# The forward scan moved to the end of the order, with an opening that starts by chunks

## The chip, the cores and the metric

One Trainium2 chip, one of its cores. The metric is the device time of one launch in microseconds, taken as the median of several runs; the profile is one further execution of the same program.

## The reference, cut to what matters

Four images of 4096 tokens with 128 channels go through two layers. The first is a state-space block with three scans over the tokens of an image: in forward order (0), backwards (1), and in an order of 16 interleaved slices (2). Each scan has 256 channels with 16 states, and its steps are sequential in time. The second layer is an attention block with 16 heads of 8 channels, then a feed-forward part and a mixture of 64 experts that each pick 8 tokens.

```python
def step(h, inp):
    u_, de_, b_, c_ = inp
    dA = jnp.exp(de_[..., None] * A)
    h = h * dA + (de_ * u_)[..., None] * b_[:, None, :]
    y = jnp.einsum('bdn,bn->bd', h, c_)
    return (h, y)
...
y = y_f + y_b + y_s
out = jnp.einsum('od,bdl->blo', out_proj_w, y)
...
x = x + _L0_conv_ref(_gn(x), ...)
t = _to_tokens(x)
t = t + _L1_attn_ref(_ln_t(t), ...)
t = t + _L1_ffn_ref(_ln_t(t), ...)
```

What matters for the change: the attention of an image needs all of its tokens, and each token needs the sum of the three scans at its place. A forward scan gives its tokens in rising order, a backward one in falling order, and the sliced one gives in each piece some tokens from all over the image.

## The kernel before, in words

The order of the work is written out by hand: Python generators issue instructions bit by bit and are advanced in turn[...]. A `Pace` advances a chain of generators by a share per turn; `flow` runs several pieces a few turns apart; `Bank` hands out a PSUM buffer (one in the main loops).

- `Inputs` makes, for each image and order, four chunks of 1024 tokens of delta, u, B and C, and the gate silu(z) (`d_sz`); it stores them in HBM. `pieces` sets the order: 0, 1, 2, with the slices laid out ahead of order 2.
- `Scans.of_image` (L488 on) runs the scan of one image in 384 steps: 3 orders x 4 chunks x 8 groups of 32 channels x 4. A step loads delta and du (L520, on SP), takes an exponential on ACT (`exp`, L534), and on DVE a product, the scan and a second product (`inputs` L541, `step` L550 and L555). Every four steps PE sums over the states (`total`, L582), and `out` (L598) adds D u and stores the group to the image's `d_y` of that order: one store on POOL for order 0 (L601), four for the others (L607, L611; for order 2 they scatter over the image). Loads are issued two steps ahead. `product` (L571 to L576) makes du for a coming chunk on the side.
- `Attention.opening` turns the sums of the scans into what the attention needs. `tokens` (L773 on) takes 512 tokens: it loads for each half of the channels the three sums and the gate (L789, on SP), adds and multiplies them on DVE (L794), multiplies by the output weights on PE (`out`, L802), adds x (L807), normalizes (`norm`, L836 to L842) and takes angles. `heads` takes the sine (L867) and `rings` makes products along a head (L879 to L886), transposes them on PE (`qT`, L894), splits them (L897, L898) and stores six parts of q on SP (L902). An opening has eight such groups of 512 tokens.
- `Attention.loop` is the attention of one image in 1024 rounds. A round has 4 score matmuls (L955), 2 exponentials of 128x1024 on ACT (L960) and 4 matmuls with the values (L969; the trace shows each as two). Behind each round it calls `beside(i)`.
- `Attention.after` closes an image: output projection, norms, feed-forward, gate logits. `settle` (L824) leaves turns empty, in number by `lag`.

The stages follow each other so. First the inputs of all images with the scan of image 0 beside them. Then the opening of image 0 in a wide form. Then the loops of images 0, 1 and 2: beside the rounds of image b, `beside` advances the scan of image b + 1 (`following`), then `after` of image b - 1 (`last`), and then, when the scan of image b + 1 is over (`left == 0.0`), the opening of image b + 1 (`opens`). What is left of the opening at the end of the loop runs in the `while not last.done or not opens.done` loop without attention rounds beside it. Last comes the loop of image 3 with the closes and the experts beside it, and the end of the experts.

In `beside`, `left` is 2.1 times the steps that the scan still has, and the scan's share per round is `left` over the rounds to 860, held between 0.5 and 1.3. While `left` is over 0, `lag` is 2 and the other work takes PE's bank only in rounds in which the scan issued an exponential and no sum (`slot`).

Of the kernel before, what the change touches and what calls it, by code (L numbers as in the profile page):

```python
# [11 lines left out]
F32 = mybir.dt.float32  # L12
# [8 lines left out]
DI = 256  # L21
NS = 16
R = 8
SLICES = 16
T = 1024
NC = L // T
NS2 = NS // 2
# [58 lines left out]
WAIT = "wait"  # L86
# [39 lines left out]
class Bank:  # L126


    def __init__(self, pool, n):
        self.pool, self.free = pool, n  # L130
# [78 lines left out]

def early(b, order, c):  # L210

    return b == 0 or (b == 1 and order == 0 and c < 2)


def decays(nc, dirs, ws, inputs):
# [12 lines left out]
class Inputs:  # L228
# [38 lines left out]
    def pieces(self, images):  # L267

        for b in images:
            self.sz[b] = self.dram.tile([DI, L], F32, name=f"d_sz_{b}")  # L270
            yield self.norm(b)
            for order in range(3):
                if order == 2:
                    yield self.slices(b)
                for c in range(NC):
                    yield self.of_chunk(b, order, c)
                    third, at = divmod(order * NC + c, 3)
                    if at == 2:
                        yield self.gate(b, third)

# [183 lines left out]
class Scans:  # L464
# [6 lines left out]
    def __init__(self, tc, ctx, ws, ident, bank, dram):  # L471
        nc = self.nc = tc.nc
        self.ws, self.bank, self.dram = ws, bank, dram
        const = ctx.enter_context(tc.tile_pool(name="s_const", side="right", bufs=1))
        self.rows = ctx.enter_context(tc.tile_pool(name="s_rows", side="right", bufs=2))
        self.deep = ctx.enter_context(tc.tile_pool(name="s_deep", side="right", bufs=3))
        self.small = ctx.enter_context(tc.tile_pool(name="s_small", side="right", bufs=2))

        self.sel = const.tile([P, 2, 32], F32, name="sel")
        nc.vector.memset(self.sel, 0.0)  # L480
        for i in range(2):
            nc.vector.tensor_reduce(
                self.sel[:, i, 16 * i : 16 * i + 16], ident.rearrange("p (d n) -> p d n", n=NS2),
                mybir.AxisListType.X, ALU.add,
            )
        self.sums, self.steps, self.did = {}, {}, set()

    def of_image(self, b, made, alone=False):  # L488

        nc = self.nc  # L490
        self.steps[b] = 0
        for order in range(3):
            self.sums[b, order] = self.dram.tile([DI, L], F32, name=f"d_y_{b}_{order}")
        steps = [(order, c, k, j) for order in range(3) for c in range(NC) for k in range(8) for j in range(4)]
        spread, ends, tiles = {}, {}, {}

        def rows_of(order, c, q):
# [61 lines left out]
        def product(s):  # L559

            order, c, k, j = steps[s]
            part, turn = divmod(4 * k + j - 8, 3)
            chunk = (b, order, c + 1) if c + 1 < NC else (b, order + 1, 0) if order < 2 else (b + 1, 0, 0)
            if part < 0 or turn == 1 or chunk not in made or early(*chunk):
                return
            of, m, at = made[chunk], part // 4, part % 4 * (T // 4)
            cut = slice(m * P, (m + 1) * P), slice(at, at + T // 4)
            if turn == 0:
                for name in ("delta", "u"):
                    t = self.extra.tile([P, T // 4], F32, tag=f"x_{name}", name=f"x_{name}_{b}_{s}")  # L570
                    nc.sync.dma_start(out=t, in_=of[name][cut])  # L571
                    tiles["x", name] = t
            else:
                t, u = tiles.pop(("x", "delta")), tiles.pop(("x", "u"))
                nc.vector.tensor_mul(t, t, u)  # L575
                nc.gpsimd.dma_start(out=of["du"][cut], in_=t)  # L576
# [10 lines left out]
        def out(s, y):  # L587

            order, c, k, j = steps[s]
            u = tiles.pop(("u", s - 3))  # L590
            o = self.rows.tile([P, T // 4], F32, tag="o", name=f"o_{b}_{s}")
            y = y[:, : T // 4]
            into = o[:, ::-1] if order == 1 else o
            if order == 2:

                into = o.rearrange("p (i j) -> p j i", i=SLICES)
                u, y = (t.rearrange("p (j i) -> p j i", i=SLICES) for t in (u, y))
            nc.vector.scalar_tensor_tensor(into, u, self.ws[order]["D"][:, k : k + 1], y, ALU.mult, ALU.add)  # L598
            to = self.sums[b, order][32 * k : 32 * k + 32]
            if order == 0:  # L600
                nc.gpsimd.dma_start(out=to[:, c * T : (c + 1) * T].rearrange("p (g t) -> g p t", g=4), in_=o)  # L601
                return
            for g in range(4):
                rows = o[32 * g : 32 * g + 32]
                if order == 1:
                    end = L - c * T - g * (T // 4)
                    nc.gpsimd.dma_start(out=to[:, end - T // 4 : end], in_=rows)  # L607
                else:
                    n = T // 4 // SLICES
                    at = (4 * c + g) * n  # L610
                    nc.gpsimd.dma_start(  # L611
                        out=to.rearrange("p (i j) -> p i j", i=SLICES)[:, :, at : at + n],
                        in_=rows.rearrange("p (i j) -> p i j", i=SLICES),
                    )
# [29 lines left out]
        for s in range(n):  # L644
            if s + self.AHEAD < n:
                yield from have(s + self.AHEAD)
            turn = s % 4 if s >= 4 else None
# [34 lines left out]
class Attention:  # L682

    def __init__(self, tc, ctx, w, gate, cols, ident, bank, dram, t1, w_out, sums, sz, x):
        nc = self.nc = tc.nc
        gate_w, gate_b = gate
        self.tc, self.cols, self.ident, self.bank, self.dram, self.t1 = tc, cols, ident, bank, dram, t1
        self.w_out, self.sums, self.sz, self.x = w_out, sums, sz, x  # L690
        const = ctx.enter_context(tc.tile_pool(name="a_const", bufs=1))
        self.half_pi = column(nc, const, math.pi / 2.0, "a_half_pi")

# [79 lines left out]
    def tokens(self, b, g, angles):  # L773


        nc = self.nc
        xin = self.x[b].rearrange("(t p) c -> p t c", p=P)
        to = self.t1[b].rearrange("(t p) c -> p t c", p=P)
        cut, tiles = slice(g * 512, (g + 1) * 512), slice(g * 4, g * 4 + 4)
        x_g = self.piece([P, 4, C], "x_g", name=f"xr_{b}_{g}")  # L780
        nc.sync.dma_start(out=x_g, in_=xin[:, tiles, :])
        ys = []
        for m in range(2):
            rows = slice(m * P, (m + 1) * P)
            parts = []
            for i, src in enumerate([self.sums[b, order] for order in range(3)] + [self.sz[b]]):
                tag, bufs = ("y0", 2 * self.n) if i == 0 else (f"p{i - 1}", self.ahead)
                t = self.one.tile([P, 512], F32, tag=tag, bufs=bufs, name=f"y{i}_{b}_{g}_{m}")
                nc.sync.dma_start(out=t, in_=src[rows, cut])  # L789
                parts.append(t)  # L790
            yield
            y = parts[0]
            for t, op in zip(parts[1:], (ALU.add, ALU.add, ALU.mult)):
                nc.vector.tensor_tensor(y, y, t, op)  # L794
            ys.append(y)
# [659 lines left out]
def tile_kernel(tc, ctx, x, in_proj_w, dirs, out_proj_w, attn, gate, weight1, weight2, out):  # L1455


    nc = tc.nc
# [26 lines left out]
                first.run(1.0)  # L1485
            others.rest()
    bank = scans.bank = Bank(ctx.enter_context(tc.tile_pool(name="bank", bufs=1, space=PSUM)), 1)
    block = Attention(tc, ctx, attn, gate, cols, ident, bank, dram, t1, w_out, scans.sums, inputs.sz, x)

    following = Pace(*(scans.of_image(b, inputs.made) for b in range(1, nb)))  # L1490
    with ExitStack() as wide:
# [11 lines left out]
    with tc.manual_schedule():  # L1503
        last = Pace()
        n = 3 * NC * NB
        for b in range(nb - 1):
            opens = Pace(block.opening(b + 1))

            def beside(i):

                left = 2.1 * (n + 1 - scans.steps.get(b + 1, 0))
                block.lag = 2 if left > 0.0 else 0
                scans.did.clear()
                following.run(min(1.3, max(0.5, left / max(1, 860 - i))))
                other = last if not last.done else opens if left == 0.0 else None
                if other is None:
                    return
                slot = left == 0.0 or "exp" in scans.did and "sum" not in scans.did
                if other.then is not PE or not bank.free:
                    other.run(1.0)  # L1520
                    slot = slot and left > 0.0
                if slot and other.then is PE and bank.free:
                    other.run(1.0)

            block.loop(b, beside)
            while not last.done or not opens.done:
                ready = scans.steps.get(b + 1, 0) > n
                if not last.done or ready:
                    (opens if last.done else last).run(1.0)
                following.run(0.5 if ready else 1.0)  # L1530
            last = Pace(block.after(b))
        following.rest()
# [69 lines left out]
```

## Time and profile before

| | us |
|---|---|
| median of 3 runs | 11980.78 (11979.94 to 11983.56) |
| profiled execution, its own time | 11985.97 |
| its span, first to last instruction | 11984.3 |
| PE busy | 10801.0 (90%) |
| ACT busy | 10457.4 (87%) |
| DVE busy | 8666.3 (72%) |
| POOL busy | 3068.7 (26%) |
| L960, exponentials of the attention, 8192 | 7778.6 busy |
| L969, matmuls with the values, 32768 | 5681.9 busy |
| mean granted TensorE clock | 0.950 |

Busy time is the union of an engine's instructions; [...] A line such as "PE out L802 <- DVE o L598" in a list of waits says that PE stood ahead of the `out` matmul of L802 until the DVE instruction of L598 was done; where several things were awaited, the last to end is named.

### The profile page before, as it was taken

The numbers are of one execution on the slowest core, as the hardware profiler recorded it, in microseconds if no ns is written. First come the engines' busy times: TensorE is split into PE (matmuls) and PEld (weight loads), VectorE is DVE, ScalarE is ACT, GpSimd is POOL, SyncE is SP. The second block draws the span as 40 slices with busy tenths as digits, with TensorE's granted clock in tenths as the row PEclk, the third lists the DMA queues.
The fourth block names the chain that finished last, engine by engine and source line by source line (L and its number), as shares of the span: only waits on it lengthen the run. The fifth ranks groups of instructions, "written<-read, shape, count | busy, mean of one in ns | idle before, by whom it ended". The sixth has DMA issues, their size and how long they took to land.

```text
span 11984.3 us, 184513 instructions
## 1 busy us (share of the span) xinstructions
PE 10801.0 (90%) x69190; PEld 3648.6 (30%) x69190; DVE 8666.3 (72%) x8841; ACT 10457.4 (87%) x10884; POOL 3068.7 (26%) x4017
## 2 busy tenths in 40 slices
PE   7898888489999999899999998999999999999995
PEld 3333333222222222233333222233332223333323
DVE  6999999889888877898889878989898321101123
ACT  5776777389999999899999988999999999999992
POOL 2323243222232322323334223233232110100011
PEclk9898989699999999999999999999999999999997
DMA  5666666655656565665565655655555332222125
GB/s 159 206 185 181 188 177 187 199 159 151 157 150 158 136 163 162 166 158 151 145 152 141 158 169 165 156 147 148 144 144 134 123 109 67 74 69 78 61 71 182
DMA packets 835831, 1747.64 MB, mean 146 GB/s; under 512 B 141070, under 2 KB 373574, under 8 KB 834678
## 3 DMA queue, kind: packets, MB, share of 16 engines
q1 hardware_dynamic: 649438, 1318.65, 41.5%
q0 software_dynamic: 144000, 307.48, 8.2%
q10 hardware_dynamic: 41496, 109.71, 3.5%
q8 instruction: 543, 8.90, 0.3%
q14 instruction: 354, 2.90, 0.1%
HBM read 1379.76 MB, written 355.47 MB: 145 GB/s over the span
## 4 chain that ended last, share of the span: by engine, by line
PE 62%; ACT 12%; issue 9%; DVE 8%; DMA 7%; SPq 1%; POOL 0%; ACTq 0%; DVEq 0%; POOLq 0%
PE acc L969 31%; PE s L955 15%; ACT e L960 7%; PE y L582 5%; DVE h L550 3%; PE cv L390 3%; PE sp L448 3%; DMA delta<-d_delta 2%; PE fo L1118 1%; PE xd L404 1%; PE h L1107 1%; DMA y<-d_y 1%; DVE dB L541 1%; ACT dA L534 1%; ACT delta L534 1%
## 5 line engine op out<-in xcount | busy, mean ns | idle before, releaser
L960 ACT ACTIVATE e<-s 128x1024 f32<-128x1024 f32 x8192 | 7778.6, 1102 | 366.5 <-PE s L955 322.0
L969 PE MATMUL acc<-e,val 128*32 128x512 f32 x32768 | 5681.9, 614 | 79.7 <-ACT av L978 79.0
L955 PE MATMUL s<-qm,key 32*128 32x512 f32 x16384 | 2783.4, 501 | 373.2 <-ACT e L960 311.5
L955 PEld LDWEIGHTS s<-qm,key 32*128 32x128 f32 x16384 | 1067.2, 183 | 3628.7 <-issue 1953.2
L552 POOL COPY ends<-h 128x1 f32<-128x1 f32 x1152 | 1299.0, 1130 | 2685.2 <-DVE h L550 2682.1
L969 PEld LDWEIGHTS acc<-e,val 128*32 128x32 f32 x32768 | 1027.7, 109 | 2007.6 <-issue 1015.7
L550 DVE TENSOR_TENSOR_SCAN h<-delta,ends,du 128x1024 f32<-128x1024 f32 x576 | 1349.6, 2343 | 113.8 <-ACT delta L534 95.9
L550 DVE TENSOR_TENSOR_SCAN h<-dA,ends,dB 128x1024 f32<-128x1024 f32 x576 | 1349.6, 2343 | 46.5 <-ACT dA L534 43.4
L541 DVE TENSOR_TENSOR dB<-du,B 128x1024 f32<-128x1024 f32 x768 | 927.8, 1208 | 603.2 <-PE y L582 387.4
L534 ACT ACTIVATE dA<-delta,A 128x1024 f32<-128x1024 f32 x768 | 938.0, 1221 | 176.9 <-DMA delta<-d_delta 169.8
L534 ACT ACTIVATE delta<-delta,A 128x1024 f32<-128x1024 f32 x768 | 939.0, 1223 | 132.7 <-PE y L582 124.6
L541 DVE TENSOR_TENSOR du<-du,B 128x1024 f32<-128x1024 f32 x768 | 920.4, 1198 | 30.4 <-DMA B<-d_bc 30.4
L555 DVE TENSOR_TENSOR du<-h,C 128x1024 f32<-128x1024 f32 x768 | 934.6, 1217 | 0.1
L555 DVE TENSOR_TENSOR dB<-h,C 128x1024 f32<-128x1024 f32 x768 | 934.2, 1216 | 0.0
L582 PE MATMUL y<-dB,sel 128*32 128x256 f32 x6144 | 724.3, 394 | 33.4 <-DVE ring L879 20.8
L582 PE MATMUL y<-du,sel 128*32 128x256 f32 x6144 | 718.1, 390 | 12.6 <-DVE du L555 12.5
L390 PE MATMUL cv<-xn,conv 128*128 128x512 f32 x1024 | 487.9, 629 | 32.5 <-DVE xn L325 17.3
L984 POOL DMA_DIRECT2D d_ctx<-av x512 | 260.1, 520 | 926.9 <-ACT av L978 920.2
L611 POOL DMA_DIRECT2D d_y<-o x512 | 329.5, 674 | 521.0 <-DVE o L598 470.7
L550 DVE TENSOR_TENSOR_SCAN h<-delta,du 128x1024 f32<-128x1024 f32 x192 | 438.2, 2282 | 19.6 <-ACT delta L534 11.0
L550 DVE TENSOR_TENSOR_SCAN h<-dA,dB 128x1024 f32<-128x1024 f32 x192 | 438.2, 2282 | 16.7 <-ACT dA L534 15.1
L576 POOL DMA_DIRECT2D d_du<-x_delta x272 | 154.7, 569 | 1104.4 <-DVE x_delta L575 1033.8
(260 smaller groups left out, 7862.8 us busy)
## 6 DMA issues: line engine op xcount, KB each, us to landing
delta<-d_delta SPq DMA_DIRECT2D x768, 512.0 KB
du<-d_du SPq DMA_DIRECT2D x576, 512.0 KB
du<-d_du ACTq DMA_DIRECT2D x192, 512.0 KB
key<-d_q SPq DMA_DIRECT2D x352, 256.0 KB
d_u<-u POOLq DMA_DIRECT2D x48, 1024.0 KB, 5.6
B<-d_bc SPq DMA_DIRECT2D x96, 512.0 KB
C<-d_bc SPq DMA_DIRECT2D x96, 512.0 KB
d_delta<-r POOLq DMA_DIRECT2D x48, 1024.0 KB, 5.5
```

Of the source, the lines that this page charges most:

```text
L390: nc.tensor.matmul(ps[:, cut], w["conv"][:, k, m * P : (m + 1) * P], reads(k, g), start=(k == 0), stop=(k == 3))
L448: nc.tensor.matmul(ps[:, cut], sign, t[:, m, cut], start=(i == 0), stop=(i == 2))
L534: nc.scalar.activation(tiles["delta", s], t, AF.Exp, scale=A)
L541: nc.vector.tensor_mul(tiles["du", s], du, spread[order, c, "B", j % 2])
L550: nc.vector.tensor_tensor_scan(h, dA, dB, first, ALU.mult, ALU.add)
L552: nc.gpsimd.tensor_copy(ends[order, c][:, at : at + 1], h[:, T - 1 :])
L555: nc.vector.tensor_mul(dB, h, spread[order, c, "C", j % 2])
L582: nc.tensor.matmul(y[32 * g : 32 * g + 32, : T // 4], self.sel[:, j // 2, :], hC[:, 256 * g : 256 * g + 256], start=(j == 0), stop=(j == 3),)
L611: nc.gpsimd.dma_start(out=to.rearrange("p (i j) -> p i j", i=SLICES)[:, :, at : at + n], in_=rows.rearrange("p (i j) -> p i j", i=SLICES),)
L955: nc.tensor.matmul(s_ps[:, k, :], keys[f"{i // 4}"][rows, cut].bitcast(F32R), queries[j, qb][rows, :].bitcast(F32R), start=True, stop=True,)
L960: nc.scalar.activation(e, s_ps, AF.Exp, scale=1.0 / math.sqrt(D))
L969: nc.tensor.matmul(accs[j, qb][32 * k : 32 * k + 32, :], v[:, k * VW : k * VW + 32], es[i][k // 2][:, k % 2, :], start=(kc == 0), stop=(kc ...
```

## The change

The order of the three scans becomes 1, 2, 0 everywhere: in the inputs, in the steps, in what `product` prepares, and in `early`. The forward scan stores each chunk of 1024 tokens in a DRAM tile of its own. `Scans` counts the groups for which `out` was issued (`stored`), and `tokens` leaves turns empty until, for its chunk c of the forward scan, two groups beyond that chunk were issued (or all 96). It then loads the sums in the order 1, 2, 0, and leaves `settle(2)` turns empty between loads and adds. In `beside` the opening may run as soon as `last` is done, where it had to wait for the end of the scan, and the rounds in which the scan is paced become 890 for 860. Each store, load, matmul and vector operation is there as often as before; line numbers after line 25 shift, by 11 at the end.

```diff
--- before.py
+++ after.py
@@ -22,6 +22,7 @@
 NS = 16
 R = 8
 SLICES = 16
+ORDERS = 1, 2, 0
 T = 1024
 NC = L // T
 NS2 = NS // 2
@@ -209,7 +210,7 @@
 
 def early(b, order, c):
 
-    return b == 0 or (b == 1 and order == 0 and c < 2)
+    return b == 0 or (b == 1 and order == ORDERS[0] and c < 2)
 
 
 def decays(nc, dirs, ws, inputs):
@@ -269,12 +270,12 @@
         for b in images:
             self.sz[b] = self.dram.tile([DI, L], F32, name=f"d_sz_{b}")
             yield self.norm(b)
-            for order in range(3):
+            for turn, order in enumerate(ORDERS):
                 if order == 2:
                     yield self.slices(b)
                 for c in range(NC):
                     yield self.of_chunk(b, order, c)
-                    third, at = divmod(order * NC + c, 3)
+                    third, at = divmod(turn * NC + c, 3)
                     if at == 2:
                         yield self.gate(b, third)
 
@@ -483,15 +484,17 @@
                 self.sel[:, i, 16 * i : 16 * i + 16], ident.rearrange("p (d n) -> p d n", n=NS2),
                 mybir.AxisListType.X, ALU.add,
             )
-        self.sums, self.steps, self.did = {}, {}, set()
+        self.sums, self.steps, self.stored, self.did = {}, {}, {}, set()
 
     def of_image(self, b, made, alone=False):
 
         nc = self.nc
-        self.steps[b] = 0
-        for order in range(3):
+        self.steps[b] = self.stored[b] = 0
+        for order in range(1, 3):
             self.sums[b, order] = self.dram.tile([DI, L], F32, name=f"d_y_{b}_{order}")
-        steps = [(order, c, k, j) for order in range(3) for c in range(NC) for k in range(8) for j in range(4)]
+        for c in range(NC):
+            self.sums[b, 0, c] = self.dram.tile([DI, T], F32, name=f"d_y_{b}_0_{c}")
+        steps = [(order, c, k, j) for order in ORDERS for c in range(NC) for k in range(8) for j in range(4)]
         spread, ends, tiles = {}, {}, {}
 
         def rows_of(order, c, q):
@@ -560,7 +563,8 @@
 
             order, c, k, j = steps[s]
             part, turn = divmod(4 * k + j - 8, 3)
-            chunk = (b, order, c + 1) if c + 1 < NC else (b, order + 1, 0) if order < 2 else (b + 1, 0, 0)
+            turn_of = ORDERS.index(order) + 1
+            chunk = (b, order, c + 1) if c + 1 < NC else (b, ORDERS[turn_of], 0) if turn_of < 3 else (b + 1, ORDERS[0], 0)
             if part < 0 or turn == 1 or chunk not in made or early(*chunk):
                 return
             of, m, at = made[chunk], part // 4, part % 4 * (T // 4)
@@ -596,10 +600,12 @@
                 into = o.rearrange("p (i j) -> p j i", i=SLICES)
                 u, y = (t.rearrange("p (j i) -> p j i", i=SLICES) for t in (u, y))
             nc.vector.scalar_tensor_tensor(into, u, self.ws[order]["D"][:, k : k + 1], y, ALU.mult, ALU.add)
+            self.stored[b] += 1
+            if order == 0:
+                to = self.sums[b, order, c][32 * k : 32 * k + 32]
+                nc.gpsimd.dma_start(out=to.rearrange("p (g t) -> g p t", g=4), in_=o)
+                return
             to = self.sums[b, order][32 * k : 32 * k + 32]
-            if order == 0:
-                nc.gpsimd.dma_start(out=to[:, c * T : (c + 1) * T].rearrange("p (g t) -> g p t", g=4), in_=o)
-                return
             for g in range(4):
                 rows = o[32 * g : 32 * g + 32]
                 if order == 1:
@@ -683,11 +689,11 @@
 
 
 
-    def __init__(self, tc, ctx, w, gate, cols, ident, bank, dram, t1, w_out, sums, sz, x):
+    def __init__(self, tc, ctx, w, gate, cols, ident, bank, dram, t1, w_out, scans, sz, x):
         nc = self.nc = tc.nc
         gate_w, gate_b = gate
         self.tc, self.cols, self.ident, self.bank, self.dram, self.t1 = tc, cols, ident, bank, dram, t1
-        self.w_out, self.sums, self.sz, self.x = w_out, sums, sz, x
+        self.w_out, self.scans, self.sums, self.sz, self.x = w_out, scans, scans.sums, sz, x
         const = ctx.enter_context(tc.tile_pool(name="a_const", bufs=1))
         self.half_pi = column(nc, const, math.pi / 2.0, "a_half_pi")
 
@@ -777,18 +783,23 @@
         xin = self.x[b].rearrange("(t p) c -> p t c", p=P)
         to = self.t1[b].rearrange("(t p) c -> p t c", p=P)
         cut, tiles = slice(g * 512, (g + 1) * 512), slice(g * 4, g * 4 + 4)
+        c, part = divmod(g, T // 512)
+        while self.scans.stored[b] < min(8 * (2 * NC + c + 1) + 2, 8 * 3 * NC):
+            yield WAIT
+        srcs = [(self.sums[b, 1], cut), (self.sums[b, 2], cut), (self.sums[b, 0, c], slice(part * 512, part * 512 + 512))]
         x_g = self.piece([P, 4, C], "x_g", name=f"xr_{b}_{g}")
         nc.sync.dma_start(out=x_g, in_=xin[:, tiles, :])
         ys = []
         for m in range(2):
             rows = slice(m * P, (m + 1) * P)
             parts = []
-            for i, src in enumerate([self.sums[b, order] for order in range(3)] + [self.sz[b]]):
+            for i, (src, cols) in enumerate(srcs + [(self.sz[b], cut)]):
                 tag, bufs = ("y0", 2 * self.n) if i == 0 else (f"p{i - 1}", self.ahead)
                 t = self.one.tile([P, 512], F32, tag=tag, bufs=bufs, name=f"y{i}_{b}_{g}_{m}")
-                nc.sync.dma_start(out=t, in_=src[rows, cut])
+                nc.sync.dma_start(out=t, in_=src[rows, cols])
                 parts.append(t)
             yield
+            yield from self.settle(2)
             y = parts[0]
             for t, op in zip(parts[1:], (ALU.add, ALU.add, ALU.mult)):
                 nc.vector.tensor_tensor(y, y, t, op)
@@ -1485,7 +1496,7 @@
                 first.run(1.0)
             others.rest()
     bank = scans.bank = Bank(ctx.enter_context(tc.tile_pool(name="bank", bufs=1, space=PSUM)), 1)
-    block = Attention(tc, ctx, attn, gate, cols, ident, bank, dram, t1, w_out, scans.sums, inputs.sz, x)
+    block = Attention(tc, ctx, attn, gate, cols, ident, bank, dram, t1, w_out, scans, inputs.sz, x)
 
     following = Pace(*(scans.of_image(b, inputs.made) for b in range(1, nb)))
     with ExitStack() as wide:
@@ -1511,9 +1522,9 @@
                 left = 2.1 * (n + 1 - scans.steps.get(b + 1, 0))
                 block.lag = 2 if left > 0.0 else 0
                 scans.did.clear()
-                following.run(min(1.3, max(0.5, left / max(1, 860 - i))))
-                other = last if not last.done else opens if left == 0.0 else None
-                if other is None:
+                following.run(min(1.3, max(0.5, left / max(1, 890 - i))))
+                other = opens if last.done else last
+                if other.done:
                     return
                 slot = left == 0.0 or "exp" in scans.did and "sum" not in scans.did
                 if other.then is not PE or not bank.free:
```

## The prediction

> **What bounds the kernel now.** I read four views: the page's busy slices, the starts of the 8192 exponentials of L960 in order, busy time by windows, and the waits by engine in those windows. L960 is a clock for the middle of the kernel: it runs twice a round, 1024 rounds an image, so activation 2048b + 2r opens round r of the attention of image b. By it the loops of images 0 to 3 run from 2436.8 to 4831.5, 4876.1 to 7248.4, 7292.1 to 9620.2 and 9621.9 to 11734.6 us. Between the loops lie tails of 44.6, 43.7 and 1.6 us in which no exponential of the attention starts. The busy windows show what kind of time each is (columns: window, its length, then busy us of PE, PEld, DVE, ACT, POOL, the granted clock, DMA share, GB/s):
>
> ```profile
> 5027.00:5469.00 442.00, 421.01 (x3020) 134.72 (x3016) 412.59 (x420) 437.18 (x471) 123.99 (x144) 0.98 0.61 155
> ...
> 4380.00:4832.00 452.00, 414.34 (x2864) 132.88 (x2860) 342.88 (x474) 418.90 (x448) 110.16 (x144) 0.96 0.59 163
> 4832.00:4876.00 44.00, 6.71 (x50) 3.28 (x46) 35.65 (x45) 6.23 (x6) 15.28 (x15) 0.58 0.73 219
> ...
> 7249.00:7292.00 43.00, 6.60 (x50) 3.26 (x46) 35.60 (x45) 6.23 (x6) 14.07 (x15) 0.61 0.71 221
> 9222.00:9620.00 398.00, 382.55 (x2562) 117.17 (x2562) 167.14 (x357) 376.27 (x405) 56.59 (x91) 0.98 0.39 119
> ```
>
> The first window has the scan of the next image and the close of the last image (`after`) beside the attention: ACT works 437.2 of 442 us. ACT is the bound there, with PE (421) and DVE (413) close behind. The second is the end of a loop, where the scan is over and the opening of the next image runs: ACT has 33 us idle, DVE over 100. The third and fourth are the tails: PE and ACT do six us of work in 44, DVE 36, at a clock of 0.6. The last is the end of loop 2, where no scan is left: rounds there take 2.05 us against 2.28 to 2.30 in an undisturbed stretch with the scan beside them, and PE is the bound. What holds the tail shows in the waits from 4380 to 4877 (who waited for whom: us, times, longest), ACT's, PE's, SP's and DVE's:
>
> ```profile
> ACT e L960 <- PE s L955: 52.7, 21, 20.3
> ACT dA L534 <- DMA delta<-d_delta: 16.9, 2, 10.9
> ...
> PE out L802 <- DVE o L598: 16.4, 3, 10.9
> PE s L955 <- DMA key<-d_q: 16.4, 1, 16.4
> PE y L582 <- DVE ring L879: 10.4, 1, 10.4
> ...
> SPq L902 <- DVE ang L897: 87.9, 7, 29.5
> ...
> DVE y L794 <- DMA y<-d_y: 22.4, 10, 7.7
> ```
>
> The last line is the start of an opening: DVE stands until a sum of the scans has come from memory, PE's `out` matmul stands behind DVE, and the attention's matmuls stand behind that one. The `key<-d_q` line is its end: the next loop's keys can't be read before the opening has stored the last of q.
>
> [...]
>
> **The change, part by part.** I counted the instruction orders of both kernels, taking L960 (L971 after) as the clock. An opening has 96 PE instructions: 64 `out` matmuls and 32 transposes.
>
> *Where the opening goes.* Before, in each of loops 0 and 1, 28 + 24 + 36 of the 96 are issued in rounds 832 to 1023 and 8 after the last round, with 32 VectorE instructions, 18 q stores and 5 exponentials of the following scan. After, loop 0 has 12, 4, 28, 20, 28 and 4 in the six stretches of 64 rounds from 640 on; loop 1 has 20, 28, 32, 16 from round 768; loop 2 has 16, 24, 40, 16. None is left past a loop's end, and behind loop 1 stand only 8 sums of the scan. Loop 2 before shows what such a boundary costs: 1.6 us. So the tails change by 1.6 − 44.6 and 2.6 − 43.7: **−84 us**. What hides the moved work is the ACT-bound time above; without that cover, its 36 us of DVE a tail come back.
>
> *Scan steps that move.* Exponentials of scans inside rounds: 410, 379, 339 before, 405, 384, 348 after: nine more (the others were in the tails). L534 takes 938.0/768 = 1.22 us, on the engine that bounds: **+11**. The slower pace (890 for 860) only spreads them: 28 in 64 rounds become 27 or 28 at first.
>
> *Stalls.* In rounds 640 to 1023 ACT idles 898 − 851.6 = 46.4 us in loop 0 (window 3933 to 4831) and 48.9 in loop 1. The last two stretches of 64 alone have 27.4 and 29.3, about 14.2 each: the opening alone, `lag` 0. The window with `after` beside the scan has 4.8 in 442, some 0.7 per 64 rounds; over rounds 64 to 767 of loops 1 and 2 it is 2.5. The opening beside the scan now gets `lag` 2, and `settle(2)` puts four turns between its loads and its adds, so the 22.4 us of DVE waiting on sums should go. Its `out` and transposes have no such pause ahead of them, so I take twice the `after` rate, 5, for four stretches, and 10 for the two in which the scan has ended: 40 a loop, **−15** for both. Bounds: −65 (2.5 throughout, 15 a loop for 46.4 and 48.9) and +75 (14.2 throughout).
>
> *VectorE as cover.* Counts times mean durations give, in the densest 96 rounds of loop 0 after (768 to 863), 233 us of DVE instructions in about 220 us. Rounds 128 to 191 of loop 2 before hold 157 by the same count; they took 148.6 us with 142.6 busy (mean durations overlap at their ends), and ACT idled 3.2. So DVE is full but not past it; I add nothing here beyond the stalls.
>
> *Loop 2.* The scan ends some 40 rounds later and shares them with the opening; those rounds were PE-bound at 2.05 us. ACT idled 29.3 us in the last 256 rounds (550 us). I take **+10**, from 0 to +28 (14.2 for 7.3 in four stretches).
>
> *Heads of loops.* After a tail the first 64 rounds have 5.9 and 8.0 us of ACT idle, loop 0's have 1.0: **−5**, from 0 to −9.
>
> *Image 0.* The scan alone, until 2201 us, has the same instructions in another order: within the reading of its 32-step stretches (159 to 195 us) I put it at 0, ±15. The opening behind it no longer waits for the last scattered stores of the slices: SP waited 4.9 us at L789 for `d_y<-o`: **−5**, from 0 to −8. The stores now go four at a time in the first two thirds; POOL is busy 26%, cost 0. The new wait on `stored` issues nothing, so nothing queues behind it on an engine; it opens chunk c two finished groups (8 steps, some 20 rounds or 46 us) after its last store was issued, against 2.2 to 9.1 us to landing. For the last chunk there is no such margin: SP may stand some 5 us, four times an image, under its lookahead.
>
> Sum: −84 + 11 − 15 + 10 − 5 − 5 = **−88 us**. Against the profiled execution's own 11985.97 (span 11984.3, 1.7 around it) that is 11898; the median of the runs, 11980.78, lies 5.2 lower, so **11893**.
>
> **Rivals.** *A, as summed: 11893, its own range 11845 to 11945.*
> *B, the stalls come along.* Every stretch with the opening idles like the opening alone, 14.2 per 64 rounds: −84 + 11 + 75 + 28 − 5 − 5 = +20, 12001. For it: `out` and the transposes wait for DVE in order, and DVE is fuller beside the scan. Against: `after` has as many bank uses beside the scan at 2.5.
> *C, the scan's loads stand behind q's stores (slower).* The six q stores of a group sit on SP and wait for DVE; delta and du for the scan two steps on stand behind them, and the exponential that waits stands ahead of the attention's on ACT. Price: the 16.9 us of `dA` waits in the tail fell on two groups, 8.5 each. Some 8, 8 and 5 groups now lie beside a scan: 21 × 8.5 = 179, with −84 + 11 − 10: +96, 12077. It decides above (84 − 11 + 10 + 24) / 21 = 5.1 us a group. For it: the L902 line. Against: from 4877 to 6797 SP stood 653.6 us behind `d_du<-x_delta`, up to 17.3 at once, and ACT waited only 24.1 us for deltas.
> *D, the opening doesn't move in time* (a bank held, `last` not done): 11981. The instruction order speaks against it.
>
> **Chances.** A 0.87, B 0.06, C 0.05, D 0.02. This kernel's measurement can tell 0.2%, 24 us, from no change. A is faster but for 0.02; B and D are within 0.2%: faster 0.85, same 0.10, slower 0.05. The range takes A's bounds and a little more: 11840 to 11950.
>
> **What would show it.** Right: tails of 1 to 4 us behind loops 0 and 1; no `PE s <- DMA key<-d_q` of 16 us; `y<-d_y` waits of DVE under 10 us a loop; ACT idle about 40 us in rounds 640 to 1023; loop 2 about 10 to 20 us longer. Wrong: ACT idle over 80 there (B), or `dA <- delta` waits over 100 us a loop with SP standing at the q stores (C). A shift of over 15 us in the scan of image 0 would make the number wrong with the mechanism right.

## The result and the profile after

The changed kernel takes 11928.0 us (median of five runs, 11922.72 to 11931.69); the kernel before, run beside it, takes 11982.81 (11979.94 to 11989.24). The ratio is 0.9954, with a 95% interval of 0.9939 to 0.9968: 0.5% faster. The forecast was 11893, with a range of 11840 to 11950.

The profiled execution took 11922.72 us with a span of 11921.0; that of before had 11985.97 and 11984.3. So the two traces differ by 63.3 us (the medians by 54.8: the traced run of the changed kernel was its fastest), and the exponentials of the attention (L960 before, L971 after) cut both spans at the same places:

| stretch of the span, us | before | after | difference |
|---|---|---|---|
| scan of image 0 and the inputs beside it, to its last exponential | 2178.2 | 2215.0 | +36.8 |
| opening of image 0, to the start of loop 0 | 258.6 | 254.0 | −4.6 |
| loop 0 | 2394.7 | 2383.9 | −10.8 |
| tail behind it | 44.6 | 1.6 | −43.0 |
| loop 1 | 2372.3 | 2360.1 | −12.2 |
| tail behind it | 43.7 | 5.8 | −37.9 |
| loop 2, with 1.6 behind it | 2329.7 | 2335.8 | +6.1 |
| loop 3 and the end | 2362.4 | 2364.7 | +2.3 |

The tails are gone, loops 0 and 1 got a little shorter and loop 2 a little longer, but the first stage, in which no attention runs, got 37 us longer. The windows of the changed kernel at the ends of the loops (window, length, then busy us of PE, PEld, DVE, ACT and POOL, granted clock, DMA share, GB/s); the first and third are rounds 640 to 1023 of loops 0 and 1, the fifth is rounds 768 to 1023 of loop 2, and the others are what is left of the tails:

```profile
3964.00:4853.00 889.00, 822.47 (x5808) 258.40 (x5804) 740.46 (x787) 856.23 (x917) 237.45 (x285) 0.98 0.62 168
4853.00:4855.00 2.00, 1.66 (x12) 0.39 (x10) 2.00 (x2) 0.95 (x2) 0.07 (x1) 1.00 0.82 153
6314.00:7215.00 901.00, 834.59 (x5920) 268.18 (x5924) 774.45 (x869) 858.18 (x919) 258.67 (x302) 0.98 0.62 168
7215.00:7220.00 5.00, 1.79 (x24) 0.76 (x18) 2.96 (x3) 1.63 (x2) 3.33 (x7) 1.00 0.40 130
8983.00:9555.00 572.00, 530.07 (x3634) 165.57 (x3628) 341.66 (x485) 532.04 (x571) 87.51 (x118) 0.96 0.48 137
```

ACT is idle for 889 − 856.23 = 32.8 us in the first window and 42.8 in the third (32.7 and 42.5 with the exact ends of the rounds); 46.4 and 48.9 were the numbers of before. DVE fills 83% and 86% of them, so it had room for the opening. In the fifth ACT idles 40.0 us. The clock of the boundaries, 0.58 and 0.61 before, is 1.00.

The waits of the changed kernel from 3963 to 4853 us, rounds 640 to 1023 of loop 0 (who waited for whom: us, times, longest):

```profile
PE s L966 <- ACT e L971: 53.3, 58, 6.1
...
ACT dA L537 <- DMA delta<-d_delta: 18.1, 8, 6.0
...
ACT e L971 <- PE s L966: 14.0, 17, 2.0
```

ACT's waits in the same rounds of the kernel before with the tail behind them, 3933 to 4877 us:

```profile
ACT e L960 <- PE s L955: 57.1, 25, 20.3
ACT dA L534 <- DMA delta<-d_delta: 26.3, 5, 10.9
```

The attention's exponential waits 14.0 us for its matmul where it waited 57.1; the 16.4 us of `s` behind `key<-d_q` are gone, and so are the 22.4 us that DVE waited for sums: there is no `y<-d_y` line in this window at all. PE now waits for ACT, which is right for a stretch that ACT bounds. ACT's wait for deltas stayed for the most part: 18.1 us for 26.3, and these 26.3 include 16.9 in the tail.

The first stage as one window, before:

```profile
0.00:2178.00 2178.00, 1841.32 (x6774) 743.37 (x6775) 1950.93 (x1506) 1530.77 (x1226) 670.01 (x820) 0.90 0.65 183
```

And after:

```profile
0.00:2215.00 2215.00, 1854.70 (x6775) 749.91 (x6776) 1952.94 (x1506) 1531.90 (x1227) 722.86 (x829) 0.90 0.64 180
```

DVE, the fullest engine of this stage, does the same 1506 instructions in 1953 us where it took 1951, and ACT one more at 1532 where it took 1531. PE is busy 13 us longer and POOL, full to a third, 53; yet the stage is 37 us longer. What was added is mostly waiting: DVE stands 2178 − 1951 = 227 us before and 262 after.

### The profile page after: what moved, and what is told of

Read it like the earlier page. It is cut to its first block, busy times and chain, and to the rows that moved or that the text cites. A ratio compares the mean times of both kernels' runs of the same rounds, so it can differ in the third digit from the quotient of the medians.

```text
span 11921.0 us, 184451 instructions
## 1 busy us (share of the span) xinstructions
PE 10787.4 (90%) x69190; PEld 3645.8 (31%) x69190; DVE 8659.3 (73%) x8841; ACT 10456.3 (88%) x10884; POOL 3206.1 (27%) x4017
## 4 chain that ended last, share of the span: by engine, by line
PE 61%; ACT 13%; DVE 9%; issue 9%; DMA 7%; POOL 0%; SPq 0%; ACTq 0%; DVEq 0%; POOLq 0%
PE acc L980 31%; PE s L966 15%; ACT e L971 7%; PE y L586 5%; DVE h L553 4%; PE cv L391 3%; DMA delta<-d_delta 2%; PE sp L449 2%; PE fo L1129 1%; PE xd L405 1%; PE h L1118 1%; DVE dB L544 1%; DMA du<-d_du 1%; ACT dA L537 1%; ACT delta L537 1%
## 5 line engine op out<-in xcount | busy, mean ns | idle before, releaser
L971 ACT ACTIVATE e<-s 128x1024 f32<-128x1024 f32 x8192 | 7773.1, 1100 | 278.9 <-PE s L966 235.5
L555 POOL COPY ends<-h 128x1 f32<-128x1 f32 x1152 | 1411.5, 1227 | 2579.1 <-DVE h L553 2575.1
```

Source lines behind the costliest of these rows:

```text
L555: nc.gpsimd.tensor_copy(ends[order, c][:, at : at + 1], h[:, T - 1 :])
L971: nc.scalar.activation(e, s_ps, AF.Exp, scale=1.0 / math.sqrt(D))
```

## Experiments

Twelve more kernels ran, each beside the kernel before on the same chip. All times are medians, ratios are to the kernel before beside them. Where two rows have different figures for before, their times differ a little by the occasion as well, and the ratios are the better comparison.

| kernel | us | before beside it | ratio, 95% interval |
|---|---|---|---|
| img0_old | 11916.45 | 11984.28 | 0.9941 [0.9929, 0.9954] |
| inputs_old | 11892.25 | 11984.28 | 0.9926 [0.9914, 0.9939] |
| order_only | 12009.47 | 11984.28 | 1.0024 [1.0016, 1.0031] |
| before_apart9 | 11986.22 | 11984.28 | 1.0003 [0.9994, 1.0011] |
| in_021 | 11907.56 | 11987.88 | 0.9933 [0.9916, 0.9949] |
| in_102 | 11908.41 | 11987.88 | 0.9937 [0.9922, 0.9952] |
| no_settle | 11956.06 | 11987.88 | 0.9974 [0.9963, 0.9985] |
| loads_pool | 11940.48 | 11987.88 | 0.9960 [0.9946, 0.9975] |
| spread_loads | 11865.08 | 11986.60 | 0.9902 [0.9887, 0.9917] |
| pace_860 | 11952.61 | 11986.60 | 0.9973 [0.9963, 0.9984] |
| spread_settle1 | 11841.80 | 11977.31 | 0.9884 [0.9869, 0.9900] |
| pace_920 | 11879.21 | 11977.31 | 0.9921 [0.9908, 0.9933] |

### Where the 37 us of the first stage come from

**img0_old** is the changed kernel with image 0 alone made and scanned in the order 0, 1, 2:

```diff
+FIRST = 0, 1, 2
-            for turn, order in enumerate(ORDERS):
+            for turn, order in enumerate(ORDERS if b else FIRST):
-        steps = [(order, c, k, j) for order in ORDERS for c in range(NC) for k in range(8) for j in range(4)]
+        steps = [(order, c, k, j) for order in (ORDERS if b else FIRST) for c in range(NC) for k in range(8) for j in range(4)]
```

> Image 0 alone goes back to the order 0, 1, 2, in its inputs and its scan; images 1 to 3 keep 1, 2, 0, in their inputs too, and all else is as changed. Open: the scan of image 0 lasts some 37 us longer in the changed kernel (last exponential at 2215 for 2178 us), and the first loop opens at 2469 for 2437. Theory T1 (image 0's own new order costs it: its scattered stores and its slices come early): the first loop opens at about 2437, and the whole takes about 11896 us. Theory T2 (the stage is sensitive to how the pieces of the inputs fall beside the scan, in all images): the opening of the first loop is moved by half of the difference or less, to 2450 or later, 11910 to 11930 in all.

The last exponential of the scan of image 0 comes at 2204.1 us: of 36.8 us, 10.9 went away with image 0's own order and 25.9 stayed. Loop 0 starts at 2462.2 and the whole takes 11916 us: T1's numbers failed, T2's came in. But T2 doesn't say what it is in the other images that counts. Their inputs are made beside this same scan, and the order of these was still 1, 2, 0.

**inputs_old** makes the inputs of every image in the order 0, 1, 2 (`enumerate(FIRST)`) and scans image 0 so; only the scans of images 1 to 3 keep the new order.

> The inputs of all images and the scan of image 0 go back to the order 0, 1, 2; the scans of images 1 to 3 keep 1, 2, 0, with the opening beside their last third. The stage of image 0 is then the one of before but for which two chunks of image 1 get their du early. T1 and T2 both: the first loop opens within 5 us of 2437 and the rest is as in the changed kernel, about 11896 us. If it stays at 2465 or more, both are wrong and the cost lies behind the scan, in the wide opening.

The stage is back: last exponential at 2178.2 us, loop 0 starts at 2437.0 (before: 2178.2 and 2436.8). The gain of the loops stayed: 2383.3, 2361.3 and 2332.5 us, tails of 1.6 and 6.2. At 11892.25 us the whole kernel stands 92 us under the one before beside it: what the prediction had forecast for the change is what this kernel gives. So by these traces 26 us are the order in which the inputs of images 1 to 3 are made, and 11 are image 0's own.

**order_only** keeps the new order and the chunked stores, and takes the rest of the change back: the opening waits for the end of the scan, the pace is 860, `settle(2)` is out.

```diff
-                following.run(min(1.3, max(0.5, left / max(1, 890 - i))))
-                other = opens if last.done else last
-                if other.done:
+                following.run(min(1.3, max(0.5, left / max(1, 860 - i))))
+                other = last if not last.done else opens if left == 0.0 else None
+                if other is None:
```

> The new order and the chunked stores stay, but the opening waits for the end of the scan again, with 860 and without the pause between loads and adds: one part of the change alone. Theory of the prediction (the gain is the two tails, and the order itself gives nothing): tails of 43 to 46 us behind loops 0 and 1 again, the stage of image 0 at +32 as in the changed kernel, 12005 to 12020 us. Rival (the order by itself helps, since the last stores of a scan no longer scatter): 11960 to 11990 us.

The tails are 43.8 and 44.7 us again, loop 0 starts at 2472.3, 35 us late, and the time is 25 us above the kernel before. The loops took back 13 us in all, hardly more than two traces of the old order differ by (before_apart9, next, has 11.5 less than before). So the order by itself costs what the stage loses, and the tails stay until the opening uses it.

**before_apart9** asks whether the stage answers in this way to any shift of the two streams against each other: the kernel before, with `flow(inputs.pieces(range(nb)), 2, 9)` for 10.

> The kernel before, with one number changed: two pieces of the inputs run 9 turns apart, where they ran 10 apart. No work is added or taken away. T1: the stage of image 0 stays within 5 us, 11978 to 11988 us in all. T2 (it is the interleaving that counts): the first loop opens 10 to 40 us away from 2437, to either side, and the whole follows.

2174.8 us and a ratio of 1.0003. One such shift moves nothing, so T2 as "any shift does it" has no support; other shifts weren't tried. Over all kernels that ran, the stage takes 2173.5 to 2181.0 us where inputs and image 0's scan have the old order (seven kernels) and 2215.0 to 2221.6 where both have the new one (four). So traces of one order differ by up to 8 us. The 26 us of the inputs stand well above that; the 11 us of image 0's own order hardly do.

**in_021** and **in_102** part the new order in two. Both are inputs_old with `enumerate(MADE if b else FIRST)`; `MADE` is 0, 2, 1 in the one (the slices, which come ahead of order 2, are made early) and 1, 0, 2 in the other (backward chunks first, slices in their old place).

> As inputs_old (image 0 wholly in the order 0, 1, 2; the scans of images 1 to 3 in 1, 2, 0), but the inputs of images 1 to 3 are made in the order 0, 2, 1: the slices come early, the chunks that read an image from its end come last. The last exponential of image 0's scan stood at 2178 us with the inputs in 0, 1, 2 and at 2204 in 1, 2, 0. Theory S (the early slices cost it): 2195 to 2210 here, 11905 to 11920 us in all. Theory R (the backward chunks first cost it, since they need the whole normalized image at once): 2178 to 2186, about 11892 to 11900 us.

> As inputs_old, but the inputs of images 1 to 3 are made in the order 1, 0, 2: the backward chunks first, the slices late as before. Theory S: last exponential of image 0's scan at 2178 to 2186, 11892 to 11900 us in all. Theory R: 2195 to 2210, 11905 to 11920 us.

The scan of image 0 ends at 2195.1 us in in_021 (+17) and at 2192.3 in in_102 (+14): either change of order costs something, and neither S nor R alone is right. As whole times the two lie 15 and 16 us above inputs_old, less than their intervals part, so the length of the stage in the trace decides here. In all these kernels the surplus is time in which DVE stands, with its work unchanged:

| first stage, us | length | DVE busy | DVE idle |
|---|---|---|---|
| before | 2178 | 1951 | 227 |
| inputs_old | 2178 | 1951 | 227 |
| in_102 | 2192 | 1952 | 240 |
| in_021 | 2195 | 1953 | 242 |
| img0_old | 2204 | 1952 | 252 |
| changed kernel | 2215 | 1953 | 262 |

The waits from 600 to 2180 us, inputs_old:

```profile
PE xt L300 <- DMA x<-in_x_dram: 15.9, 4, 4.8
PE cv L392 <- DVE xn L327: 15.2, 3, 5.6
...
DVE dB L545 <- PE y L587: 38.7, 18, 4.7
...
DVE h L554 <- issue: 10.6, 5, 4.2
```

in_102:

```profile
DVE dB L546 <- PE y L588: 43.3, 17, 5.1
...
PE xt L301 <- DMA x<-in_x_dram: 23.7, 7, 7.3
...
PE cv L393 <- DVE xn L328: 21.8, 3, 7.7
```

and in_021:

```profile
DVE dB L546 <- PE y L588: 48.7, 22, 5.8
...
DVE h L555 <- issue: 20.2, 8, 4.3
```

In in_102 PE waits 7.8 us longer at the norm of an image (`xt`) for x and 6.6 us longer at the convolution (`cv`) for the normalised rows. Together that is 14.4 us, as much as the stage lost, but PE isn't the fullest engine here, and that these waits carry the loss isn't shown. In in_021 those two are almost unchanged (16.8 and 15.2 us). There DVE waits 10 us longer at `dB` for PE's sums and 10 us longer before `h` ("issue": the profile shows nothing that it waited for), and ACT's `xds` behind `xd` 20 us longer (119.9 for 99.5); waits of several engines in one chain can't be summed. In the changed kernel, over its whole first stage, the two waits of DVE are 57.4 and 23.2 us where they were 40.2 and 11.3 before: 29 of its 35 us. That the order 0, 2, 1 costs some 17 us and the order 1, 0, 2 some 14 is shown; that it is the early slices or the early backward chunks as such, and what makes DVE stand, is not.

### The pause between an opening's loads and its adds

**no_settle** is the changed kernel without the line `yield from self.settle(2)`.

> The changed kernel without the four empty turns between the loads of the scans' sums and their adds: one part undone. The theory of the prediction (the turns keep DVE from standing before sums that have not come): DVE waits for d_y of 15 to 30 us a loop, ACT idle in rounds 640 to 1023 of loops 0 and 1 up by 10 to 25 us each, 11945 to 11980 us. Rival (the loads have come anyway, since DVE runs behind what is issued): within 5 us of 11928.

11956.06 us, 28 above the changed kernel (24 by the ratios). The waits in rounds 640 to 1023 of its loop 1:

```profile
DVE y L804 <- DMA y<-d_y: 27.8, 10, 10.5
ACT dA L537 <- DMA delta<-d_delta: 27.4, 8, 7.0
```

The same lines of the changed kernel, its loop 1 from 6314 to 7215 us:

```profile
ACT dA L537 <- DMA delta<-d_delta: 19.7, 5, 10.4
...
DVE y L805 <- DMA y<-d_y: 9.4, 2, 9.2
```

In rounds 640 to 1023 of the three loops DVE's waits for sums grow from 0, 9.4 and 15.2 us to 14.3, 27.8 and 15.4, and ACT's idle time from 32.7, 42.5 and 47.9 to 36.0, 64.8 and 60.5. That the pause is worth some 24 to 28 us, nearly all in loops 1 and 2, is shown. The reason given for it holds in loop 1, where both grow together, by 18 and 22 us. In loop 0 DVE waits 14 us longer for sums and ACT loses only 3; in loop 2 ACT loses 13 while the sums are awaited as long as before. Without the pause an opening also falls on other rounds (that of loop 2 fills 192 from round 768 on, where it fills 256 with the pause), and how much of the loss comes of that no run tells.

### What ACT still waits for: deltas behind the opening's loads

Late deltas, as rival C had them, are in the trace in small. Over the three loops ACT waited 28.1, 24.1 and 27.6 us for deltas before, and 38.4, 30.2 and 37.7 after. SP's issues ahead of one such stall, changed kernel (start, length, engine, line, transfer):

```profile
6601.69 3.88 SPq L799 DMA_DIRECT2D y<-d_y  x3
6608.28 0.32 SPq L799 DMA_DIRECT2D y<-d_sz  x1
6609.56 1.27 SPq L799 DMA_DIRECT2D y<-d_y  x3
6611.11 0.32 SPq L799 DMA_DIRECT2D y<-d_sz  x1
...
6613.11 0.55 SPq L523 DMA_DIRECT2D delta<-d_delta  x1
```

and ACT at its end:

```profile
6624.00 1.15 ACT L537 ACTIVATE dA<-delta,A 128x1024 f32<-128x1024 f32 x1 [10.44 <-DMA delta<-d_delta]
```

Eight loads of 128x512 float32, two megabytes, go out in ten microseconds; the delta behind them (512 KB, with a load of keys and one of values in between) is issued at 6613.1 and used at 6624.0, 10.9 us later, and ACT stands 10.44 of them. SP isn't held by q stores here, as C had it. The DMA engines are nearly full in this time (the last two numbers are their busy share and GB/s):

```profile
6615.00:6620.00 5.00, 0.10 (x2) 0.00 (x0) 0.00 (x0) 0.00 (x0) 2.77 (x6) 0.66 0.98 255
6620.00:6625.00 5.00, 0.00 (x0) 0.00 (x0) 0.00 (x0) 1.00 (x1) 0.00 (x0) 0.50 0.87 228
```

Either the delta stands behind these loads on SP's queue (Q), or it shares the DMA engines with them (M).

**loads_pool** tells these apart: the changed kernel with the opening's loads issued by GpSimd (`by = nc.gpsimd if self.n == 2 else nc.sync`).

> The changed kernel with the loads of the sums and the gate of the openings of images 1 to 3 issued by POOL, where SP issues them. Open: in rounds 640 to 1023 ACT still stands 18 to 20 us a loop before deltas, up to 10.4 at once, and SP stands 28 to 48 us a loop at these loads. Theory Q (the delta stands behind those loads on SP, in order): waits of ACT for deltas in these rounds fall below 8 us a loop, 11890 to 11915 us. Theory M (they share the DMA engines, and two megabytes at once are in the way wherever they are issued): the waits stay at 15 us or more, within 15 us of 11928, or above it where POOL's own stores come late.

ACT's waits for deltas in rounds 640 to 1023 of the three loops are 13.1, 17.8 and 15.0 us, against 18.1, 19.7 and 24.2, and the time is no better (11940.48). Loop 1:

```profile
DVE y L806 <- DMA y<-d_y: 24.1, 6, 13.4
ACT dA L537 <- DMA delta<-d_delta: 17.8, 4, 8.8
```

With the loads on another engine's queue 46 of 62 us stay, nearly twice what Q allowed, so Q isn't the main cause; but a quarter of the wait did go, and M's 15 us a loop was missed in loop 0. DVE's wait for sums in loop 1 rose from 9.4 to 24.1 us, which takes the gain back. The 46 of 62 us that stayed agree with M, but this run by itself doesn't show that the delta and the loads share the DMA engines.

**spread_loads** takes the burst apart, on inputs_old: one load a turn.

```diff
                 parts.append(t)
+                if self.lag:
+                    yield
```

> As inputs_old (11892), but while the scan runs the four loads of a half (three sums and the gate, 256 KB each) are issued one a turn, where they are issued together. Issuing them from POOL left ACT's waits for deltas where they were, so they don't come of the order on SP. Theory M (a delta shares the DMA engines with a megabyte or two issued at once): ACT's waits for deltas in rounds 640 to 1023 fall from about 18 to under 9 us a loop, 11860 to 11885 us. Rival N (these waits belong to the chunk ends and the loads of B and C, not to the opening): they stay within 5 us a loop and the time within 12 us of 11892.

11865.08 us, 27 under inputs_old. Rounds 640 to 1023 of loop 1 in inputs_old:

```profile
ACT dA L538 <- DMA delta<-d_delta: 21.8, 4, 10.5
...
DVE y L806 <- DMA y<-d_y: 9.0, 2, 8.7
```

and in spread_loads:

```profile
DVE y L808 <- DMA y<-d_y: 2.1, 4, 0.6
...
ACT dA L538 <- DMA delta<-d_delta: 10.2, 4, 6.0
```

In these rounds of the three loops the deltas cost 6.9, 10.2 and 13.4 us where they cost 18.1, 21.8 and 21.3: 31 us less. N falls; M's bound of 9 us was met in loop 0 alone, but its direction and the time came in. Loads issued apart stand apart on SP's queue too, so it is this run and loads_pool together that speak for M. The three loops got 43 us shorter. It costs something as well: the opening takes more turns, and a tail of 29.6 us, 23 more than in inputs_old, came back behind loop 1.

**spread_settle1** therefore shortens the pause, `settle(1)` for `settle(2)`, since the spread loads already stand apart from their adds.

> As spread_loads (11865), with two empty turns between loads and adds where it has four. In spread_loads the four turns of loads came on top of the pause, the opening in loop 1 ran over the end of the loop, and a tail of 29.6 us came back; here the instruction order has nothing of an opening past a loop. If the loads one a turn give the time that the sums need: that tail under 7 us, the waits for deltas and sums as in spread_loads, 11835 to 11850 us. If the pause itself was needed: DVE waits for d_y up by over 15 us a loop and no gain, 11860 to 11885.

The tail behind loop 1 is 1.6 us again (5.9 behind loop 0), loops take 2367.5, 2347.9 and 2324.4, and the whole 11841.8 us: a ratio of 0.9884, 135 us under the kernel before beside it. It is the fastest version that ran, and beats both kernels.

### The pace of the scan

**pace_860** and **pace_920** are inputs_old with 860 and 920 in place of 890.

> As inputs_old (11892), but the scan is paced to end at round 860 again, where the change says 890: one part undone. Theory of the prediction (the pace only spreads the steps, ACT being full either way): within 12 us of 11892, tails under 7 us. Rival (the later end is what gives the opening its room): the opening is pressed into rounds with less cover, ACT idle in rounds 640 to 1023 up by 10 us a loop or more, 11910 to 11930.

> As inputs_old (11892), with the scan paced to end at round 920. At 860 it took 11953, with 67 us more of ACT idle over the three loops, 39 of it before deltas, though the numbers of scan steps and opening instructions in each 64 rounds are nearly the same. Theory V (fewer scan steps a round leave room, and this goes on): 11870 to 11895, waits for deltas over the loops no more than the 107 us at 890. Theory W (it is how loads, stores and steps happen to meet, with no trend in the pace): anywhere from 11880 to 11950, with deltas not following the pace.

At 860 the time is 11952.61 us, 60 above inputs_old (56 by the ratios), with tails of 2.7 us: the tails go without the slower pace, but two thirds of the gain don't come. Loop 1, rounds 640 to 1023:

```profile
ACT dA L538 <- DMA delta<-d_delta: 39.0, 7, 11.1
```

The wait was 21.8 us at 890. Over the loops ACT idles 252.5 us where it idled 185.6, 67 more, and 39 of those are waits for deltas. In each 64 rounds the scan's exponentials differ by three at most in loops 0 and 1, and in loop 1 the opening falls almost as it did; in loop 0 it begins sooner (the traces show 64 of its 160 PE instructions by round 768, where they showed 32), so the expectation for 920 is wrong to call its counts nearly the same there. Rounds 768 to 831 of loop 0 take 178.0 us with 28.0 of ACT idle, against 154.7 and 5.7. At 920 the time is 11879.21; loop by loop it changes by −27, +10 and +12, so this one step past 890 shows no trend. Why three per cent of pace costs 60 us on one side and nothing on the other stays partly open: the deltas are 39 of the 67 us, and nothing that was run parts the rest. Whether the kernel before would gain from 890 by itself wasn't tried, so how much of the gain is the pace's alone stays open.

## Why the prediction was right, and its number 35 us off

By the steps of its sum; a loop's length is ACT's busy and idle time in it.

1. *Where the opening goes, −84.* Measured −43.0 − 37.9 = −80.9. Counting instructions against the attention's exponential placed the opening rightly, and order_only, where the opening waits for the scan again, has the tails back; only the eight sums of the scan behind loop 1 took 5.8 us, not 2.6.
2. *Scan steps that move, +11.* The counts are those of the trace (five fewer in loop 0, five more in loop 1, nine more in loop 2). The price is too high. ACT's busy time in the three loops changed by −4.3, +4.0 and +7.8 us: 0.8 to 0.9 us a step, where 1.22 is the mean duration of one. Durations that overlap at their ends add up to more than the busy time (in loop 0 before, all of ACT's to 2882 us for 2326.5 busy). So +7.5, not +11.
3. *Stalls, −15.* ACT's idle time in rounds 640 to 1023 went from 46.4 and 48.9 to 32.7 and 42.5: −20. Forecast were 40 each. That this came so near is luck in part. before_apart9, with the loops of before, has 40.3 and 45.2, and order_only, in which the opening runs alone with `lag` 0 and no pause, has 36.4 and 41.2. So most of the drop can't be put down to `lag` and the pause, the reason given. What no_settle shows is the other side: without the pause the moved opening would have brought 36.0 and 64.8.
4. *The slower pace "only spreads them", at no cost.* Wrong as a reason: on inputs_old the step from 860 to 890 is worth 60 us. The pace was part of the change, so the forecast of stalls escaped; that was luck. As an estimate, were the step worth as much on the changed kernel, at 860 it would have taken 11928 + 60 = 11988 us, no faster than before.
5. *VectorE as cover, 0.* Held: DVE's 740 of 889 and 774 of 901 us, and ACT's idle time fell.
6. *Loop 2, +10, and heads, −5.* ACT's idle time in its last 256 rounds rose from 29.3 to 39.5, the +10 as put. The heads gave more than twice their size: from 5.9 and 8.0 us of idle to 0.0 and 1.9, −12.
7. *Image 0: "the scan alone has the same instructions in another order: I put it at 0, ±15".* **This step failed.** It measured +36.8. The instructions of the scan are indeed the same, but it isn't alone: the inputs of images 1 to 3 are made beside it, and the change reorders these too, which the step left out. That part is 26 us, shown by img0_old against inputs_old; image 0's own order is 11, of the size of the ±15 and hardly above the scatter of the traces. The opening behind the scan gave the −5 that was put on it.

With the terms as measured: tails −80.9, loops −16.9, image 0 +32.2, loop 3 and the end +2.3 make −63.3, the difference of the spans. The sum forecast −88; the tails were 3 short and the loops 18 better than it had them, image 0 was 37 worse. That is 25 of the 35 us. The other 10 are the steps between a trace and a median, 5 on either side: 5.2 were taken off for the median of before, and the traced run of the changed kernel lay 5.3 under its own median. The loops' 18 aren't the prediction's to claim: before_apart9 came out 11.5 better in its loops with no such change.

Of the rivals, B (stalls come along) would have had ACT idle over 80 us; no_settle comes nearest, at 64.8 in loop 1. C (deltas late) exists at 26 us over the three loops, not 179, and, as far as loads_pool and spread_loads tell, through the DMA engines more than through SP's queue: of the waits in rounds 640 to 1023, 46 of 62 us stayed with the opening's loads on another queue, and 31 of 61 with them issued one at a time. D didn't occur. The prediction named a shift of over 15 us in the scan of image 0 as what would spoil the number with the mechanism right, and that is what happened.

## What to carry to other kernels

Here a drain between two stages was worth nearly its whole length (81 of 88 us), because its work fitted beside a stage that another engine bounds (in rounds 640 to 1023 of loop 0 ACT was busy 856 of 889 us, DVE 740), and counting instructions against a steady one told ahead of the run where it would land. A change of order has to be priced at every place that reads the constant: here it moved the making of inputs too, and keeping the old order there, changing only the scans of images 1 to 3, won another 36 us. A reason for a gain is best tested on a run that lacks it: order_only already shows most of the drop in stalls that `lag` and the pause were to explain. Three settings of a stream beside another one were each worth a run here: its loads in small pieces (27 us, spread_loads), the pause before their use (24 to 28 us for having it, no_settle; 23 for halving it once the loads were spread, spread_settle1), and the pace, on both sides (60 us lost at 860, none at 920).

## What the runs showed of the hardware

A load of 512 KB issued just behind two megabytes was used 10.9 us after its issue, and the 16 DMA engines were 98% and 87% busy in the two stretches of 5 us before its use. Issuing the two megabytes from another engine lowered the sum of such waits, in rounds 640 to 1023 of three loops, from 62 to 46 us; issuing them one at a time, on inputs_old, halved it from 61 to 31. In a stage of 2178 us in which DVE was busy 1951, another order of the same work left DVE standing 262 us for 227. And an ACT instruction of 1.22 us mean duration, moved into a full stretch, added 0.8 to 0.9 us of busy time.
